# Attention and graph convolution in float32 on one core: the values' bias moved to VectorE between products, and the second half of the next x loaded into a place of the numerators

## The chip, the cores and the metric

The kernel runs on one core of one Trainium2 chip. The metric is the device time of one execution in microseconds (us), the median of the runs shown. One execution was also recorded by the hardware profiler; every instant below is in us from the start of its span. The engines are TensorE (PE; its weight loads are PEld), VectorE (DVE), ScalarE (ACT), GpSimd (POOL) and SyncE (SP), which only issues DMAs here.

## The reference

32 graphs of 512 nodes with 512 features pass through two layers, each with a residual and a layer norm:

```
q, k, v = x @ Wq + bq, x @ Wk + bk, x @ Wv + bv          # 8 heads of 64
scores  = q @ k.T / 8 + (-1e9 where adj == 0)
x = layernorm(x + softmax(scores) @ v)
norm_adj = adj * deg^-0.5[:, None] * deg^-0.5[None, :]   # deg = adj.sum(axis=1)
x = layernorm(x + norm_adj @ (x @ weight) + bias)
```

`x` is 32 x 512 x 512 in float32 and `adj` 512 x 512. Everything below is in float32 or in a high and a low part of it.

## The kernel before

`unshifted` does the work; `general` is a second version that runs only where a test at the end says that the first one's numbers left their bounds. The batch index is `b`, one graph at a time, and the two layers of different graphs are overlapped. Iteration `b` of the main loop is four stages on TensorE:

1. `stretch(b, one)`: scores of two pairs of heads, their exponentials, and the product with the values (tiles `sc`, `e`, `av`). Eight numerators `e` of 128 x 1024 lie in `NUM`; each stretch uses all eight in order, so the eighth, `NUM[:, 7]`, is written last.
2. Keys and queries of graph `b + 1` (`k0` and `k1`, 14 products taken in turn), with the layer norms of graphs `b - 1` and `b - 2` beside them.
3. `stretch(b, two)`: the other two pairs of heads.
4. `main` of 22 pieces: four of `first` (adjacency times graph `b - 1`), the values of graph `b + 1`, and `second` (times the weight of layer two).

The large products are computed with seven multiplications in place of eight (`seven` with tables such as `CHAIN`, `LEAF`, `OUTER`), from sums and differences of blocks. Those of x are made by GpSimd in `XT` by `combine` (four) and `quarters` (four more), after VectorE has transposed the two halves of x into `XT` (`turn(b, 0)` and `turn(b, 1)`). In stage 4 the values are six leaf products, a seventh, a sum on GpSimd (`spread_last`), and three outer products at positions 13, 15 and 17 of `main`; the seven products of `second` are at 10, 14, 16 and 18 to 21. The step at position n of `main` is followed by what `beside` has under n. Each of the tables' products writes a PSUM bank; the three outer ones all write the same one, region "A", and ScalarE or VectorE takes each result out (`put`, `add`) into `V[b]` or `y`. Region "A" of `second` serves its products 1, 3, 5 and 7.

Instructions keep the order in which the program names them on each engine (`keep_in_program_order`); DMAs are issued from SP in an order that the scheduler sets, and each waits at the head of the queue for what it needs. An instruction waits by semaphores for the others that write what it reads or read what it writes.

The values' bias: `bias_values(b)` adds `bv_r` to the four rows of `V[b]`, four additions of 128 x 512 on GpSimd. They stand at position 18, behind the eight combinations of x. On GpSimd the sums of numerators of the next stretch (`accumulate`, tile `acc`, six additions of 128 x 1024) follow, and behind those the roots of a layer norm (`rstd`, `add`), for which ScalarE's `store` waits (tile `y`). `store` and the evictions of keys and queries (`kq`) alternate on ScalarE.

x is loaded in two halves, four DMAs each. Both use one buffer, `x`, so the second half (`load_x(b, 1)`, called from `turn(b, 0)`) starts after the first has been transposed. Only for graph 1 does the second half lie in `NUM[:, 7]`.

Outputs of a stretch leave PSUM by a transpose on VectorE into `yb`, one buffer, and four DMAs each into `YT` (`yT<-yb`). `swap` exchanges the weights of queries and values in one tile, `wqv`.

Of the kernel before, what the change touches and what calls it, by code (L numbers as in the profile page):

```python
# [50 lines left out]
def unshifted(  # L51
# [15 lines left out]
    B, N, D = x.shape  # L67
    NT = N // P
# [5 lines left out]
    tensor, vector, scalar, gpsimd = (InOrder(tc, e) for e in (nc.tensor, nc.vector, nc.scalar, nc.gpsimd))  # L74
# [24 lines left out]
    def each(f, *args):  # L99
        return [lambda a=a: f(*a) if isinstance(a, tuple) else f(a) for a in args]  # L100

    def run(pieces):
        for f in pieces:
            f()

    def play(main, beside=None):
        for n, f in enumerate(main):
            f()
            run((beside or {}).get(n, ()))
# [11 lines left out]
        return NUM[:, next(taken) % 8]  # L121

    def load_x(b, j):
        if b == 1 and j == 1:
            X[b, j] = NUM[:, 7].rearrange("p k (n t r) -> p (k n) t r", t=DT, r=32)
        else:
            X[b, j] = acts.tile([P, 8, DT, 32], F32, name="x", bufs=1)
        for q in range(4):
            nc.sync.dma_start(
                X[b, j][32 * q : 32 * (q + 1)],  # L130
                x[b, ts(j, HALF), ts(q, P)].rearrange("(k s) (t r) -> s k t r", s=32, r=32),
            )

    def turn(b, j):
        vector.transpose(
            XT[:, 2 * j : 2 * j + 2].rearrange("p i u (k s) -> p (i u) k s", s=32),
            X.pop((b, j)).rearrange("p k t r -> p t k r"),
        )
        if j == 0 and b > 1:
            load_x(b, 1)  # L140

    turned = {}

# [75 lines left out]
    def load_row(v, name, engine):  # L219
        t = consts.tile([P, v.shape[0]], F32, name=name)  # L220
        engine.dma_start(t, bass.AP(tensor=v.tensor, offset=v.offset, ap=[[0, P], [1, v.shape[0]]]))
        return t
# [9 lines left out]
    for i in range(2):  # L232
# [3 lines left out]
        if i == 0:  # L236
            bv_r = load_row(bv, "bv_r", nc.scalar)
# [130 lines left out]
    KQ, V = {}, {}  # L368
# [50 lines left out]
        leaf = seven(LEAF, multiply_quarters, put_quarters, add_quarters, (4, P))  # L419
        return leaf + [spread_last] + seven(OUTER, multiply, put, add)  # L420

    def bias_values(b):
        for n in range(NT):
            gpsimd.tensor_add(V[b][:, n, :], V[b][:, n, :], bv_r)

    def keys_and_queries(b, r):
        def multiply(p, i, j, fresh):
            for c, w in enumerate((wk, wqv)):
                for u in range(2):
                    tensor.matmul(  # L430
                        p[:, c, :], w[:, i, u, ts(r, P)], XT[:, j, u, :],
                        start=fresh and c == 0 and u == 0, stop=u == 1, skip_group_check=True,
                    )

        def out(i, j):
            if (b, ORDER[0]) not in KQ:
                for g in ORDER:
                    KQ[b, g] = acts.tile([P, 2, N], F32, name="kq", bufs=6)
            return KQ[b, r + 2 * i][:, :, ts(j, HALF)]

        def put(q, p):
            g = r + 2 * q[0]
            for c in range(2):
                scalar.activation(out(*q)[:, c], p[:, c], AF.Identity, bias=bias[:, c, g : g + 1], scale=1.0)

        def add(q, p):
            vector.tensor_add(out(*q), out(*q), p)

        return seven(CHAIN if b else PLAIN_FIRST, multiply, put, add)
# [367 lines left out]
    v = values_of(0)  # L817
# [13 lines left out]
    weigh_quarters(gpsimd)  # L831
    nc.sync.dma_start(stored[1], NUM[:, :4].rearrange("p e k (u o) -> p (e k) u o", u=2)[:, :7])
    nc.sync.dma_start(stored[0], wqv)
    bias_values(0)
    play(keys_and_queries(0, 1), {
        1: [lambda: adjacency(0)], 3: [lambda: turn(1, 0), lambda: adjacency(1)],
    })
# [8 lines left out]
    for b in range(B):  # L846
        one, two = ORDER[:2], ORDER[2:]
        f[b], c[b] = finish(b), convolve(b)
        ahead, back = f.get(b - 1), c.get(b - 2)
        if 1 < b < LAST:  # L850
            load_residual(b - 1)
        if b + 2 < B:
            load_x(b + 2, 0)
        if b == LAST:
            load_residual(b)
        stretch(b, one, back["measure"][:3] if back else ())

        def folds(gs):
            return [[lambda g=g, b=b: fold(b, g)] for g in gs]

        def turns(b=b + 2):
            if b >= B:
                return [], [], []
            return [lambda: turn(b, 0)], [lambda: turn(b, 1)], [lambda k=k: combine(b, k) for k in range(4)] + [quarters]

        fold0, fold1 = folds(one) if b < LAST else ([], [])
        rest = back["measure"][3:] + back["root"] if back else []
        store = back["store"] if back else []
        if b < LAST:
            k0, k1 = keys_and_queries(b + 1, 0), keys_and_queries(b + 1, 1)  # L870
            main = [p for pair in zip(k0, k1) for p in pair]
            if b == 0:
                exact = each(compare, *range(NT))
                weights = each(lambda k: weigh_part(w1, gpsimd, k), *range(4))
                beside = {
                    1: fold0, 2: [degrees], 3: weights[:1], 4: fold1, 5: weights[1:2] + exact[:1], 6: exact[1:2],
                    7: weights[2:3], 8: exact[2:3], 9: weights[3:], 10: exact[3:],
                }
            else:
                measure, norm, low = ahead["measure"], ahead["norm"], ahead["low"]  # L880
                scale = ahead["inverse"] + ahead["scale"] if b == 1 else []
                beside = {
                    0: rest + scale + ahead["add"], 1: store[:1] + fold0, 2: store[1:2], 3: store[2:3] + fold1,
                    4: store[3:] + measure[:2], 5: measure[2:] + ahead["root"], 7: norm[:1] + ahead["judge"],
                    8: norm[1:2] + low[:1], 9: norm[2:3] + low[1:2], 10: norm[3:] + low[2:3],
                    11: low[3:] + ahead["lift"],
                }
            play(main, beside)
        else:
            e = f[b]  # L890
            conv = c[b - 1]
            play(conv["first"], {
                0: rest + store[:1] + conv["parts"][:0], 1: store[1:2] + ahead["judge"] + conv["parts"][:1],
                2: store[2:] + e["sums0"],
                3: conv["parts"][1:] + e["inverse0"] + ahead["grow"],
            })

        if b < LAST:
            swap(1)
        stretch(b, two, f[b]["pairs"][0] + f[b]["pairs"][1] if b == LAST else ())  # L900

        fold0, fold1 = folds(two) if b < LAST else ([], [])
        turn0, turn1, combined = turns()
        if b < LAST:
            end = f[b]
            v, bias_v = values_of(b + 1), [lambda b=b + 1: bias_values(b)]
            back_to_queries = [lambda: swap(0)] if b < LAST - 1 else []
            if b == 0:
                play(v, {
                    1: fold0, 4: fold1, 8: turn0, 9: turn1, 10: combined + back_to_queries + bias_v,  # L910
                })
            else:
                conv = c[b - 1]
                second = conv["second"]
                k = 6 if b < LAST - 1 else 8
                main = conv["first"] + v[:k] + second[:1] + v[k:9] + second[1:2] + v[9:10] + second[2:3] + v[10:] + second[3:]
                grow, parts, scale = ahead["grow"], conv["parts"], end["scale"]
                if b < LAST - 1:
                    beside = {
                        1: parts[:1] + fold0, 3: parts[1:], 5: fold1, 6: grow[:1], 8: grow[1:2], 9: grow[2:3] + end["inverse"],  # L920
                        10: grow[3:] + scale[:1], 11: scale[1:2], 13: turn0 + scale[2:3], 14: scale[3:],
                        16: turn1, 17: combined[:2], 18: combined[2:] + back_to_queries + bias_v,
                    }
                else:
                    measure, norm, low = end["measure"], end["norm"], end["low"]
                    beside = {
                        0: [lambda: load_residual(LAST - 1)], 1: parts[:1] + fold0, 3: parts[1:], 5: fold1,
                        6: grow[:1], 8: grow[1:2], 9: end["inverse"], 10: grow[2:3] + scale[:2], 11: grow[3:] + scale[2:] + end["add"],
                        14: measure[:1], 15: measure[1:2], 16: measure[2:3],
                        17: measure[3:] + end["root"], 18: norm[:1] + bias_v, 19: norm[1:2] + low[:1], 20: norm[2:3] + low[1:2],  # L930
                        21: norm[3:] + low[2:] + end["lift"],
                    }
                play(main, beside)
# [312 lines left out]
```

## Time and profile before

| | |
|---|---|
| median of 3 runs | 2786.29 us (2782.73 to 2787.06) |
| the profiled execution | 2788.38 us, its span 2786.6 us |
| granted TensorE clock | 0.995 |
| one iteration in the middle, from one restart of TensorE in stage 2 (1015.90) to the next (1100.97) | 85.07 us |
| TensorE's products of stage 4 in that iteration | 1040.55 to 1071.84 |
| scores and av after it | 1071.84 to 1085.93 |
| keys and queries | 1085.93 to about 1111.5 |
| the additions `v<-v,bv_r` on GpSimd | 128, 1300 ns each in the mean, 161.8 us |
| GpSimd's additions of 128 x 1024, `acc<-acc,e` | 248, 2373 ns each |
| VectorE's turn of half an x, `xT<-x` | 61, 1242 ns each |

A profile line gives the start, the time, the engine, the operation and what it writes and reads, its shape and count; in square brackets is how long the engine sat idle before it and what ended that. In the list of waits the numbers are us in total, how often, and the longest. In the chain of waits each step is what released the next. Ends of TensorE's products are modelled: a group of four is shown longer than the distance to the next one.

### The profile page before, as it was taken

Reading aid. Unit: us, or ns where it says so; the run is one execution under the profiler, and the core shown is the slowest. Engines: PE = TensorE matmul, PEld = TensorE weight load, DVE = VectorE, ACT = ScalarE, POOL = GpSimd, SP = SyncE. Lnnn points to the kernel's source line nnn. Section 1 sums busy time; section 2 is a strip of 40 time slices with the busy share of each in tenths; the row PEclk is TensorE's granted clock in tenths of the full one; section 3 lists DMA queues with packets and bytes.
Section 4 is the critical chain, followed back from the end, with each engine's and each line's share of the span. In section 5 each row is a group of like instructions: output and inputs, shape, how many; then the busy total and the mean of one; then the engine's idle time right before and its main releaser. Section 6 shows DMA issues by size and latency. Waiting matters only on the chain.

```text
span 2786.6 us, 36220 instructions
## 1 busy us (share of the span) xinstructions
PE 2717.3 (98%) x13284; PEld 1907.6 (68%) x13284; DVE 1972.3 (71%) x2809; ACT 1257.0 (45%) x1807; POOL 1999.4 (72%) x1335
## 2 busy tenths in 40 slices
PE   9899999999999999999999999999999999999997
PEld 6566766766767667667667676676676676766765
DVE  4767767677676777776676767777777767677777
ACT  3344434454344544344543445443545434454444
POOL 5667676687776776766877767767668777677674
PEclk9999999999999999999999999999999999999999
DMA  5213333233333233332333332333323333323321
GB/s 178 80 45 109 99 86 101 77 94 106 88 98 103 61 111 90 95 102 74 97 106 88 96 99 68 110 88 94 106 68 103 106 87 95 96 71 110 93 59 47
DMA packets 388187, 256.76 MB, mean 92 GB/s; under 512 B 278816, under 2 KB 346400, under 8 KB 379936
## 3 DMA queue, kind: packets, MB, share of 16 engines
q1 hardware_dynamic: 386848, 252.78, 30.5%
q8 instruction: 107, 1.75, 0.3%
q10 hardware_dynamic: 1152, 1.57, 0.2%
q14 instruction: 80, 0.66, 0.1%
HBM read 183.77 MB, written 37.22 MB: 79 GB/s over the span
## 4 chain that ended last, share of the span: by engine, by line
PE 76%; DVE 8%; POOL 5%; ACT 4%; DMA 3%; SPq 2%; issue 1%; ACTq 0%; DVEq 0%; POOLq 0%
PE mm L45 48%; PE sc L45 15%; PE av L45 13%; POOL acc L45 2%; ACT kq L45 2%; DMA yT<-yb 2%; SPq L512 2%; ACT y L45 1%; DVE yb L45 1%; DVE folded L45 1%; DVE acc L45 1%; DVE ve L45 1%; POOL rstd L45 1%; POOL xT L45 1%; DVE st L45 1%
## 5 line engine op out<-in xcount | busy, mean ns | idle before, releaser
L45 ACT ACTIVATE e<-e 128x1024 f32<-128x1024 f32 x512 | 541.3, 1057 | 599.6 <-DVE e L45 566.7
L45 DVE SCALAR_TENSOR_TENSOR e<-sc,maskT 128x1024 f32<-128x1024 f32 x512 | 584.9, 1214 | 64.6 <-PE sc L45 64.6
L45 POOL TENSOR_TENSOR acc<-acc,e 128x1024 f32<-128x1024 f32 x248 | 588.5, 2373 | 19.4
L45 PE MATMUL mm<-xT,wk 128*128 128x256 f32 x1792 | 466.5, 383 | 32.5 <-ACT kq L45 32.5
L45 POOL TENSOR_TENSOR xT<-xT 128x512 f32<-128x512 f32 x250 | 314.2, 1273 | 243.2 <-DVE xT L45 233.4
L45 PE MATMUL sc<-kq 64*128 64x512 f32 x2048 | 459.8, 597 | 2.8 <-DVE e L45 1.4
L45 PE MATMUL av<-e,v 128*64 128x512 f32 x2048 | 456.9, 598 | 5.2 <-POOL v L45 4.9
L45 PE MATMUL mm<-xT,wqv 128*128 128x256 f32 x1792 | 459.9, 379 | 0.0
L45 PEld LDWEIGHTS mm<-xT,wk 128*128 128x128 f32 x1792 | 334.9, 190 | 113.4 <-ACT kq L45 44.1
L45 PEld LDWEIGHTS mm<-xT,wqv 128*128 128x128 f32 x1792 | 340.5, 190 | 46.3
L45 PEld LDWEIGHTS av<-e,v 128*64 128x64 f32 x2048 | 145.3, 137 | 309.4 <-issue 232.4
L45 PEld LDWEIGHTS sc<-kq 64*128 64x128 f32 x2048 | 191.8, 186 | 238.9 <-issue 182.0
L45 ACT ACTIVATE kq<-mm,bias 128x256 f32<-128x256 f32 x512 | 213.9, 472 | 234.7 <-PE mm L45 232.1
L45 PE MATMUL mm<-wqv,xT 128*128 128x128 f32 x1736 | 304.8, 322 | 5.8 <-DVE v L45 5.8
L45 POOL TENSOR_TENSOR acc<-e 128x1024 f32<-128x1024 f32 x126 | 298.1, 2366 | 17.4 <-ACT e L45 17.4
L45 POOL TENSOR_TENSOR yT<-yT,b_r 128x512 f32<-128x512 f32 x126 | 157.2, 1281 | 212.4 <-DVE lo L45 212.4
L45 PEld LDWEIGHTS mm<-wqv,xT 128*128 128x128 f32 x1736 | 263.4, 192 | 30.0 <-issue 4.6
L45 DVE STREAM_TRANSPOSE yb<-av 128x512 f32<-128x512 f32 x127 | 91.1, 717 | 259.4 <-DMA yT<-yb 191.9
L45 DVE TENSOR_TENSOR v<-v,mm 128x512 f32<-128x512 f32 x221 | 147.5, 679 | 151.0 <-PE mm L45 146.3
L45 PE MATMUL mm<-w,zT 128*128 128x256 f32 x992 | 229.5, 379 | 0.0
L45 DVE STREAM_TRANSPOSE acc<-acc 128x1024 f32<-128x1024 f32 x124 | 152.6, 1231 | 77.1 <-POOL acc L45 76.8
L45 PEld LDWEIGHTS mm<-w,zT 128*128 128x128 f32 x992 | 186.1, 190 | 24.8 <-issue 0.8
(133 smaller groups left out, 3446.6 us busy)
## 6 DMA issues: line engine op xcount, KB each, us to landing
wqv<-wv_parts SPq DMA_DIRECT2D x31, 1792.0 KB, 7.5
wqv<-wq_parts SPq DMA_DIRECT2D x30, 1792.0 KB, 7.5
yT<-yb SPq DMA_DIRECT2D x508, 64.0 KB, 2.3
x<-in_x_dram SPq DMA_DIRECT2D x244, 128.0 KB, 3.2
out_dram<-y SPq DMA_DIRECT2D x120, 256.0 KB, 2.0
xr<-in_x_dram SPq DMA_DIRECT2D x118, 256.0 KB, 3.6
wk<-in_x_dram SPq DMA_DIRECT2D x8, 256.0 KB, 2.8
wv_parts<-e SPq DMA_DIRECT2D x1, 1792.0 KB, 7.6
```

The source lines that it names most:

```text
L45: return self.tc.keep_in_program_order(op(*args, **kwargs))
L512: nc.sync.dma_start(YT[b][:, :, (4 * g + q) * 32 : (4 * g + q + 1) * 32], yb[32 * q : 32 * (q + 1)],)
```

## The change

Three things change in iterations of the main loop.

- `turn` no longer loads the second half. `load_x(b + 2, 1)` is called once in iteration `b`, after `stretch(b, two)`, and puts the second half into `NUM[:, 7]`, for every graph.
- `bias_values` adds one row and takes an engine. For the values of graphs 2 to 30, iterations 1 to 29, VectorE adds the four rows, after positions 17, 18, 19 and 20 of `main`, each in front of an addition of `second`. In iterations 0 and 30 and for graph 0 GpSimd still does it.
- In iterations 1 to 29 the second turn moves from position 16 to 14, ahead of the last scaling and of the addition of the second outer product. GpSimd's combinations follow it after 14, 15 and 17; `swap(0)` goes from 18 to 17.

```diff
@@ load_x @@
-        if b == 1 and j == 1:
+        if j == 1:
             X[b, j] = NUM[:, 7].rearrange("p k (n t r) -> p (k n) t r", t=DT, r=32)
@@ turn @@
             X.pop((b, j)).rearrange("p k t r -> p t k r"),
         )
-        if j == 0 and b > 1:
-            load_x(b, 1)
@@ bias_values @@
-    def bias_values(b):
-        for n in range(NT):
-            gpsimd.tensor_add(V[b][:, n, :], V[b][:, n, :], bv_r)
+    def bias_values(b, n, engine=gpsimd):
+        engine.tensor_add(V[b][:, n, :], V[b][:, n, :], bv_r)
...
-    bias_values(0)
+    run(each(bias_values, *((0, n) for n in range(NT))))
...
         turn0, turn1, combined = turns()
+        if b + 2 < B:
+            load_x(b + 2, 1)
         if b < LAST:
             end = f[b]
-            v, bias_v = values_of(b + 1), [lambda b=b + 1: bias_values(b)]
+            v, bias_v = values_of(b + 1), each(bias_values, *((b + 1, n) for n in range(NT)))
...
                 if b < LAST - 1:
+                    bias_v = each(bias_values, *((b + 1, n, vector) for n in range(NT)))
                     beside = {
                         1: parts[:1] + fold0, 3: parts[1:], 5: fold1, 6: grow[:1], 8: grow[1:2], 9: grow[2:3] + end["inverse"],
-                        10: grow[3:] + scale[:1], 11: scale[1:2], 13: turn0 + scale[2:3], 14: scale[3:],
-                        16: turn1, 17: combined[:2], 18: combined[2:] + back_to_queries + bias_v,
+                        10: grow[3:] + scale[:1], 11: scale[1:2], 13: turn0 + scale[2:3], 14: turn1 + scale[3:] + combined[:1],
+                        15: combined[1:2], 17: combined[2:] + bias_v[:1] + back_to_queries, 18: bias_v[1:2],
+                        19: bias_v[2:3], 20: bias_v[3:],
                     }
```

## The prediction

> **What bounds the kernel now.** I read the page first, then the waits, the chain of waits over one middle batch, and each engine's timeline over that batch (iteration 11's values, then iteration 12's keys and queries). Busy time of the engines, from the page:
>
> ```profile
> PE 2717.3 (98%) x13284; PEld 1907.6 (68%) x13284; DVE 1972.3 (71%) x2809; ACT 1257.0 (45%) x1807; POOL 1999.4 (72%) x1335
> ```
>
> TensorE is the bound: only 69 us of the span are left to win unless products change, and none do. What TensorE waits for (sum, times, longest):
>
> ```profile
> PE mm L45 <- ACT kq L45: 32.5, 29, 1.6
> PE mm L45 <- DVE v L45: 5.8, 4, 3.6
> PE av L45 <- POOL v L45: 4.9, 1, 4.9
> ```
>
> One wait in each of 29 batches holds half of it. The chain of waits shows where it comes from (start, length):
>
> ```profile
> 1092.89 2.35 POOL acc L45
> 1095.23 0.98 POOL rstd L45
> ...
> 1098.06 0.70 ACT y L45
> 1098.76 0.73 ACT kq L45 x2
> 1099.49 0.70 ACT y L45
> 1100.19 0.74 ACT kq L45 x2
> 1100.93 0.04 issue
> 1100.97 10.63 PE mm L45 x48
> ```
>
> GpSimd's sums of the numerators (acc) end late, the root (rstd) queues behind them, ScalarE's first output row (y) waits for the root, and the keys' evictions (kq) queue behind y. The ninth product of the stage wants the bank that the fifth one's eviction empties. GpSimd's timeline says why acc is late:
>
> ```profile
> 1065.56 10.36 POOL L45 TENSOR_TENSOR xT<-xT 128x512 f32<-128x512 f32 x8 [6.96 <-DVE xT L45]
> 1075.88 4.98 POOL L45 TENSOR_TENSOR v<-v,bv_r 128x512 f32<-128x512 f32 x4
> 1080.83 2.37 POOL L45 TENSOR_TENSOR acc<-e 128x1024 f32<-128x1024 f32 x1
> ```
>
> The numerators were there from about 1076.5 (ScalarE's exponentials begin at 1074.28, 1.12 apart, two are needed). Acc begins at 1080.83 because of x's late second half and the bias.
>
> **What the Trainium skill says.** "SBUF — State Buffer", section "Who interferes with whom": a VectorE instruction with two SBUF inputs and a GpSimd instruction that reads SBUF exclude each other, and the later one waits for the whole of the other. The bias on VectorE is such an instruction. The trace agrees; the timeline of the first batch has the same shape, 128x512 from two SBUF inputs, beside four GpSimd additions:
>
> ```profile
> 79.57 5.86 POOL L45 TENSOR_TENSOR w<-w 128x512 f32<-128x512 f32 x4
> 80.25 1.15 DVE L45 TENSOR_TENSOR plainT<-plainT,adjT 128x512 f32<-128x512 f32 x1
> 82.62 1.67 DVE L45 TENSOR_TENSOR plainT<-plainT,adjT 128x512 f32<-128x512 f32 x1
> 86.12 0.69 DVE L45 TENSOR_TENSOR plainT<-plainT,adjT 128x512 f32<-128x512 f32 x1
> ```
>
> Alone it takes 0.69. Beside GpSimd it ends some 0.56 after GpSimd's addition: the first of the four ends at 79.57+1.27=80.84, VectorE at 80.25+1.15=81.40. The second, held back by about 0.46, ends near 82.57, and VectorE, which comes at 82.62, just misses that gap and waits for the third: 1.67. GpSimd's next one, held back, takes about 1.72 (the first v,bv_r additions, from 28.59, last 3.39 for two beside VectorE's) instead of 1.27.
>
> **The change, part by part.** VectorE's order around the outer products decides (v are the values' additions from PSUM, y the second factor's):
>
> ```profile
> 1058.20 0.69 DVE L45 TENSOR_TENSOR v<-v,mm 128x512 f32<-128x512 f32 x1 [0.73 <-PE mm L45]
> 1058.81 1.24 DVE L45 STREAM_TRANSPOSE xT<-x 128x1024 f32<-128x1024 f32 x1
> 1059.97 0.65 DVE L45 TENSOR_TENSOR yT<-yT,inv 128x512 f32<-128x512 f32 x1
> 1060.54 0.68 DVE L45 TENSOR_TENSOR y<-yT,mm 128x512 f32<-128x512 f32 x1
> 1061.14 0.68 DVE L45 TENSOR_TENSOR yT<-yT,inv 128x512 f32<-128x512 f32 x1
> 1061.74 0.68 DVE L45 TENSOR_TENSOR v<-v,mm 128x512 f32<-128x512 f32 x1
> 1063.31 0.69 DVE L45 TENSOR_TENSOR y<-yT,mm 128x512 f32<-128x512 f32 x1 [0.90 <-PE mm L45]
> 1064.17 1.25 DVE L45 STREAM_TRANSPOSE xT<-x 128x1024 f32<-128x1024 f32 x1 [0.17 <-DMA x<-in_x_dram]
> ```
>
> *The load.* Four DMAs of 128 KB into the eighth numerator. They wait for GpSimd's last sum of that place, which ends at 1045.7 (six sums from 1031.16), not for the first turn, and land near 1053 (3.2 from issue to landing). In the built order of the SP queue two of them stand ahead of the second four yT<-yb transfers, which before went out at 1043.2. These now leave after 1046.6 and land before 1052; they are wanted by the first scaling at 1056.2. That cover of 4 us makes it cost nothing. Were acc to end 5 us later, it would show. swap(0) and the residual wait for TensorE (1065.0, 1072.1) as before.
>
> *The second turn earlier.* It goes from 1064.17 to 1061.17, straight behind y, then the last scaling, then the addition of the second outer product at 1061.17+1.16+0.60=1062.93 instead of 1061.74. That addition has a customer: all three outer products use one bank, and the third product waits for it (the same wait, 0.85, stands twice in the first batch, at 119.82 and 122.67, each 0.75 after its addition began). The third product begun at 1063.11; it will begin at 1062.93+0.75=1063.68. **Loss 0.57 per batch**, 29 x 0.57 = 16.5 us. Nothing hides it: TensorE has no other work in its order.
>
> *GpSimd.* The eight xT combinations start near 1062.9; the third waits for the third outer product (about 1065.7). With the bias interleaved they end near 1075, and 4.98 us of bias are gone. Acc can begin when the exponentials permit, 4.3 us earlier than at 1080.83 on the same scale. The root then starts near 1091.3 instead of 1095.2; ve, which needs GpSimd to be between two sums, is ready at 1089.4 and ends by 1091.2. First y at 1092.7, then kq, y in turn (0.72 each): the fifth kq ends near 1097. TensorE needs it at 1099.8. **The wait goes whole**, with 2.8 us to spare. Its worth: idle 32.5/29=1.12, and 0.16 that the modelled ends hide (groups of four matmuls start 0.865 apart: 1098.98+0.865=1099.84, next start 1100.97, so 1.13 lost where 0.97 is shown): 29 x 1.28 = 37.2 us. Next on that path would be the product itself.
>
> *The bias on VectorE.* 29 x 4 additions of 0.69. Between the y additions, one per TensorE product of 1.73, 1.04 are free. Against GpSimd's additions each pair runs as a cycle: GpSimd held back 1.72, VectorE's bias ending 0.56 after the boundary, y in between. 1.72 fits 1.73. So what counts is whether the first bias catches the boundary between the third and fourth combination. Counted from the third outer product's end E: VectorE starts the third product's two v additions at E+0.20 (its y starts 0.20 after each product, 1068.49 for 1068.29), they last 1.25, and bias needs their result (0.04 more, as between a turn of acc and its sum), so it is ready at E+1.49. GpSimd's third combination starts between E+0.22 and E+0.31 (parts started 0.31 after the last product that reads its place) and ends at E+1.49 to E+1.58. Caught, on the scale of this batch with the 0.57 of delay in it: the four biases end at 1067.55, 1069.30, 1071.03 and 1072.77, the last y at 1073.37, and the scores permit e at 1073.59 (1073.02+0.57): cost 0. Missed: each of them is some 1.2 later, the y of the fifth product of the second factor ends at 1071.1, and the seventh, which adds to the same bank and would start at 1070.6, starts 0.55 late: 29 x 0.55 = 16 us. Both ends kept; I take caught, since a GpSimd start of 0.31 is what the trace has.
>
> *First batch.* GpSimd keeps its bias there, but the second turn waited 2.41 for x. It comes 2.5 earlier, and so do the bias and the av products that waited 4.9 for it: gain 2.5 us (the wait of sc is upstream of it and not added).
>
> Sum on the profiled execution (2788.4 us, span 2786.6): 2788.4 - 37.2 + 16.5 - 2.5 = 2765.2. The median of the runs is 2.1 below that execution: **2763 us**.
>
> **Rivals.**
> - *The boundary is missed.* 16 us more: 2779. For it: a tie within 0.1 us. Against: the 0.31 above.
> - *The outer product does not wait*, because VectorE gets there sooner than my addition of rows: 2763 - 16.5 = 2747. Against: the rows are 0.6 pitched throughout.
> - *A convoy at the shared port: slower.* If held-back GpSimd additions take 1.9 instead of 1.72, a bias-y cycle exceeds the 1.73 of a product and lateness adds up, 0.2 a turn; with a missed boundary the last y and e come some 0.9 late. The scores have little slack: e pitch 1.14 against 0.88 for a pair of products, four pairs of banks to run ahead in. Price 0.57+0.55+0.9=2.0 a batch, 58 us, against gains of 39.7: 2786.3+18=2804. It decides from 1.37 us a batch. For it: nearly touching schedules; against: 1.71 to 1.74 where the two engines alternated.
> - *No change*: the missed boundary with a larger outer wait (1.3 a batch), about 2785.
>
> **How the numbers follow.** Caught boundary 0.48, missed 0.24, no outer wait 0.08, no change 0.08, convoy 0.12. 0.2% (5.6 us, about what a measurement of this kernel can tell) puts the missed case mostly, not wholly, among the faster ones. Faster 0.76, same 0.12, slower 0.12. Range 2746 to 2783.
>
> **What will show it.** PE mm <- ACT kq gone from the waits; a PE mm <- DVE v of about 0.4 to 0.6, 29 times; v<-v,bv_r on DVE with a mean near 1.15 (0.56 after the boundary), 1.2 to 1.7 for the first one if missed; xT on POOL with a mean near 1.5; acc starting 4.7 after the first scores. I am wrong if kq's wait stays, if sc waits for DVE e, or if yT<-yb's new place on SP shows up before a scaling.

## The result and the profile after

The changed kernel takes 2761.62 us (median of 6 runs, 2760.66 to 2762.93), the kernel before beside it 2785.93 (6 runs). The ratio is 0.9915, with a 95% interval from 0.9902 to 0.9928: 0.85% faster. The profiled execution took 2760.92 us, its span is 2759.1.

The busy line of the page of the changed kernel, then two lines from its list of what TensorE waited for (total, times, longest):

```profile
PE 2715.4 (98%) x13284; PEld 1907.3 (69%) x13284; DVE 2075.0 (75%) x2925; ACT 1259.6 (46%) x1807; POOL 1910.7 (69%) x1219
```

```profile
PE mm L45 <- DVE v L45: 15.2, 33, 3.6
...
PE av L45 <- POOL v L45: 4.0, 2, 3.8
```

TensorE's own work is the same. The line for ScalarE's kq, 32.5 us in 29 batches before, is gone from the list. In its place the wait for VectorE's v has risen from 4 occurrences to 33: a new one in each of the same 29 batches, 0.32 us shown each time. VectorE's busy time rises by 103 us and GpSimd's falls by 89, and neither is the bound.

GpSimd's timeline of the changed kernel in the same iteration 11 (start, time, operation; in brackets the idle time before it):

```profile
1051.10 2.90 POOL L45 TENSOR_TENSOR xT<-xT 128x512 f32<-128x512 f32 x2 [3.92 <-DVE xT L45]
...
1054.26 9.36 POOL L45 TENSOR_TENSOR xT<-xT 128x512 f32<-128x512 f32 x6 [0.25 <-PE mm L45]
...
1065.71 2.37 POOL L45 TENSOR_TENSOR acc<-e 128x1024 f32<-128x1024 f32 x1 [2.10 <-ACT e L45]
```

The sums of numerators now wait for ScalarE's exponentials for 2.10 us, where before they came late. They begin 4.70 us after the first scores (1061.01); before it was 8.99 (1080.83 against 1071.84). So ScalarE's alternation of y and kq starts early too. Two lines from its timeline in the changed kernel:

```profile
1081.57 0.82 ACT L45 ACTIVATE y<-y,add,rstd 128x512 f32<-128x512 f32 x1 [1.87 <-POOL add L45]
...
1085.12 0.84 ACT L45 ACTIVATE kq<-mm,bias 128x256 f32<-128x256 f32 x2
```

The second of them is the fifth eviction of keys and queries. It ends at 1085.96; the ninth product of the stage, which needs its bank, starts at 1089.02. There are 3 us to spare where there was a wait.

The chain of waits shows what has become late instead (start, length of each step):

```profile
1046.79 0.69 DVE v L45
1047.47 1.00 DVE xT L45
...
1048.58 0.62 DVE yT L45
1049.20 0.60 DVE y L45
1049.80 0.40 DVE xT L45
...
1050.88 0.65 DVE yT L45
1051.53 0.61 DVE v L45
...
1052.18 8.90 PE mm L45 x40
```

Reading from the bottom: TensorE's third outer product starts at 1052.18, released by VectorE's addition of the second one, which stood behind a scaling, the second turn, y, another scaling and the first turn, without a gap. TensorE's own timeline in the same stretch:

```profile
1049.97 1.89 PE L45 MATMUL mm<-w,parts 128*128 128x256 f32 x8
1052.18 1.99 PE L45 MATMUL mm<-wqv,xT 128*128 128x256 f32 x8 [0.32 <-DVE v L45]
1054.01 1.89 PE L45 MATMUL mm<-w,zT 128*128 128x256 f32 x8
```

Without the wait the outer product would have started one pitch, 1.73 us, after the one before it: 1049.97 + 1.73 = 1051.70. So it is 0.48 late, of which the list shows 0.32, because the modelled end of the product before it hides the rest.

Last, VectorE's and GpSimd's meeting at the bias (VectorE's timeline):

```profile
1054.21 1.28 DVE L45 TENSOR_TENSOR v<-v,mm 128x512 f32<-128x512 f32 x2 [1.49 <-PE mm L45]
...
1055.53 0.69 DVE L45 TENSOR_TENSOR v<-v,bv_r 128x512 f32<-128x512 f32 x1
...
1056.14 0.68 DVE L45 TENSOR_TENSOR y<-y,mm 128x512 f32<-128x512 f32 x1
1056.74 1.16 DVE L45 TENSOR_TENSOR v<-v,bv_r 128x512 f32<-128x512 f32 x1
...
1061.18 0.67 DVE L45 TENSOR_TENSOR y<-yT,mm 128x512 f32<-128x512 f32 x1
...
1062.19 4.62 DVE L45 SCALAR_TENSOR_TENSOR e<-sc,maskT 128x1024 f32<-128x1024 f32 x4 [0.34 <-PE sc L45]
```

GpSimd's third combination begins at 1054.26 and, at its 1.27, ends at 1055.53. This end is the boundary of which the prediction speaks. The first bias begins at that very instant and takes 0.69, as if alone; GpSimd's fourth combination begins 0.08 later, at 1055.61. So it is in all 29 batches. The next three biases take about 1.16, each waiting for the end of one combination. The last y ends at 1061.85, 0.34 before e can begin: the scores are not delayed.

### The profile page after: what moved, and what is told of

It is laid out like the page before. It is cut to its first block, busy times and chain, and to the rows that moved or that the text cites. A ratio compares the mean times of both kernels' runs of the same rounds, so it can differ in the third digit from the quotient of the medians.

```text
span 2759.1 us, 36196 instructions
## 1 busy us (share of the span) xinstructions
PE 2715.4 (98%) x13284; PEld 1907.3 (69%) x13284; DVE 2075.0 (75%) x2925; ACT 1259.6 (46%) x1807; POOL 1910.7 (69%) x1219
## 3 DMA queue, kind: packets, MB, share of 16 engines
q8 instruction: 107, 1.75, 0.3%
## 4 chain that ended last, share of the span: by engine, by line
PE 90%; DVE 7%; issue 1%; POOL 1%; ACT 0%; DMA 0%; SPq 0%; DVEq 0%; POOLq 0%; ACTq 0%
PE mm L45 58%; PE av L45 16%; PE sc L45 16%; DVE xT L45 2%; DVE yT L45 2%; DVE v L45 2%; DVE y L45 1%; POOL xT L45 0%; DVE st L45 0%; DVE lo L45 0%; ACT yT L45 0%; ACT hi L45 0%; DVE e L45 0%; POOL y L45 0%; DMA xr<-in_x_dram 0%
## 5 line engine op out<-in xcount | busy, mean ns | idle before, releaser
L45 POOL TENSOR_TENSOR xT<-xT 128x512 f32<-128x512 f32 x250 | 369.0, 1486 | 156.9 <-DVE xT L45 139.8
L45 PE MATMUL mm<-wqv,xT 128*128 128x128 f32 x1736 | 306.5, 322 | 15.2 <-DVE v L45 15.2
L45 PE MATMUL mm<-adjT,hi 128*128 128x512 f32 x512 | 201.6, 397 | 0.8 <-ACT e L45 0.8
```

The source lines that it names most:

```text
L45: return self.tc.keep_in_program_order(op(*args, **kwargs))
```

## The experiments

Seven kernels were run, each beside the kernel before (2786.05 and 2786.32 in the two groups). The edits are shown against the changed kernel, that of e2 against the kernel before; `...` stands for code that is left out. The table has the time, what TensorE waited for in the profile (shown us, times), and how long after the first scores of one middle batch acc began.

| kernel | us (runs) | <- ACT kq | <- DVE v | <- DVE y | acc after scores |
|---|---|---|---|---|---|
| before | 2785.93 (6) | 32.5, 29 | 5.8, 4 | none | 8.99 |
| the change | 2761.62 (6) | none | 15.2, 33 | none | 4.70 |
| e1 bias back on GpSimd | 2760.00 (4) | none | 15.1, 33 | none | 5.91 |
| e2 bias alone | 2750.48 (4) | none | 6.0, 4 | 1.2, 4 | 5.46 |
| e3 turn one place later | 2762.46 (4) | none | 5.9, 4 | 9.8, 28 | 4.75 |
| e4 short sum ahead of the bias | 2762.00 (4) | none | 15.2, 33 | none | 4.70 |
| e5 bias and load, turn where it was | 2743.48 (4) | none | 6.0, 4 | none | 5.23 |
| e6 load alone | 2771.46 (4) | 20.9, 29 | 5.9, 4 | none | 8.71 |
| e7 longer sum ahead of the bias | 2784.60 (12) | none | 15.2, 33 | 14.4, 29 | 4.75 |

**e1: is it the bias leaving GpSimd that pays?**

```diff
-                    bias_v = each(bias_values, *((b + 1, n, vector) for n in range(NT)))
-                        15: combined[1:2], 17: combined[2:] + bias_v[:1] + back_to_queries, 18: bias_v[1:2],
-                        19: bias_v[2:3], 20: bias_v[3:],
+                        15: combined[1:2], 17: combined[2:] + back_to_queries, 18: bias_v,
```

> The change with the four additions of the bias put back on GpSimd behind the combinations of x; the early load and the early second turn stay. My theory: what matters is only that the sums of numerators start at least 1.3 us sooner than before. GpSimd's combinations now end about 7.8 us after the third of them starts, the bias about 5 us later, so acc starts some 6.1 us after the first scores, where it was 9.0 before and is 4.7 in the change. That is enough: PE mm <- ACT kq stays at zero, PE mm <- DVE v stays near 0.3 shown (0.5 in truth) in 29 batches, time 2762 (2759 to 2766), the same as the change. Rival, that the bias leaving GpSimd is what pays: kq's wait comes back in part or whole, 2775 to 2799.

It took 2760.00, ratio to before 0.9904 (0.9888 to 0.9921), against 0.9915 (0.9902 to 0.9928) for the change: the intervals of the ratios overlap, so no difference is claimed. GpSimd's timeline of this run:

```profile
1054.17 7.78 POOL L45 TENSOR_TENSOR xT<-xT 128x512 f32<-128x512 f32 x6 [0.24 <-PE mm L45]
1061.90 4.97 POOL L45 TENSOR_TENSOR v<-v,bv_r 128x512 f32<-128x512 f32 x4
1066.83 2.37 POOL L45 TENSOR_TENSOR acc<-e 128x1024 f32<-128x1024 f32 x1
```

Six combinations that nobody holds back take 7.78, not 9.36, and the bias 4.97 more; acc begins only 1.2 later, relative to the scores, than in the change. That is still early enough, and the wait for kq stays away. With x turned early, the bias need not leave GpSimd at all. The rival falls.

**e2: the bias alone.** x is loaded and turned as in the kernel before, and the four rows of the bias go to VectorE as in the change (`bias_values` and its other calls are those of the change too).

```diff
+                    bias_v = each(bias_values, *((b + 1, n, vector) for n in range(NT)))
...
-                        16: turn1, 17: combined[:2], 18: combined[2:] + back_to_queries + bias_v,
+                        16: turn1, 17: combined + bias_v[:1] + back_to_queries, 18: bias_v[1:2],
+                        19: bias_v[2:3], 20: bias_v[3:],
```

> The kernel before with the bias alone moved to VectorE between the second factor's products; x is loaded and turned as before. My theory: acc starts about 3 us sooner than before (GpSimd's eight combinations, four of them held back by 0.46, end near 12.1 us after their start, and no bias follows), so PE mm <- ACT kq is gone; and the second outer product's addition is not delayed, so PE mm <- DVE v is back at 4 occurrences. Gain 37 of before: 2749 (2746 to 2753), faster than the change by 12. Rival, that the additions on VectorE cost what they delay (PSUM banks freed late, e late): 2760 or more, with PE sc <- DVE or PE mm <- DVE y waits in every batch.

It took 2750.48 (2748.10 to 2752.27), ratio 0.9871 (0.9855 to 0.9888): inside what was expected, and faster than the change. Each of the two moves, the early turn in e1 and the bias here, removes the wait for kq by itself; the one of the bias does so without the new wait for v.

**e3: the second turn one place later**, behind the second outer product's addition.

```diff
-                        ... 14: turn1 + scale[3:] + combined[:1],
-                        15: combined[1:2], 17: combined[2:] + bias_v[:1] + back_to_queries, 18: bias_v[1:2],
+                        ... 14: scale[3:],
+                        15: turn1 + combined[:2], 17: combined[2:] + bias_v[:1] + back_to_queries, 18: bias_v[1:2],
```

> The change with the second turn moved one place later, from behind position 14 to behind 15, so that the second outer product's addition comes before it. My theory: the third outer product no longer waits for it, 29 x 0.5 = 14 us back: 2748, with PE mm <- DVE v at 4 occurrences. But the first bias now comes within 0.1 us of GpSimd's boundary behind its second combination; if it misses, the seventh product of the second factor starts some 0.5 late and the time is 2762 again, with PE mm <- DVE y 29 times. Rival, that the wait for DVE v hides something else that ends just as late: about 2760 with another wait in its place.

It took 2762.46, the time of the change, but not by the same wait: the one for v is back at 4, and one for y stands in 28 batches. Its timeline, both engines and TensorE:

```profile
1053.31 11.80 POOL L45 TENSOR_TENSOR xT<-xT 128x512 f32<-128x512 f32 x8 [5.11 <-DVE xT L45]
...
1055.95 1.75 DVE L45 TENSOR_TENSOR v<-v,bv_r 128x512 f32<-128x512 f32 x1
...
1060.13 1.97 PE L45 MATMUL mm<-w,zT 128*128 128x256 f32 x8 [0.35 <-DVE y L45]
```

GpSimd starts its combinations at a moment that is bad for the bias: its third one begins at 1055.89, 0.06 before the bias, which then waits for all of it and takes 1.75. The y behind it come later, and the seventh product of `second` waits for the fifth one's addition to their common bank. This was the second outcome named in the expectation.

One of the 29 batches of this run went the other way, and it is the test of the boundary within one kernel:

```profile
295.92 0.83 DVE L45 TENSOR_TENSOR v<-v,bv_r 128x512 f32<-128x512 f32 x1
```

There the combination on GpSimd had still 0.28 us to run when the bias asked. The bias took 0.83 instead of 1.74 to 1.76, TensorE did not wait for y, and from the scores behind the batch before it to those behind it 83.92 us went by, against 84.48 to 84.57 for the 27 batches that follow. GpSimd starts some 0.3 later in the same batch of e2 and e5 too; why was not found out.

**e4 and e7: does the boundary decide?** A sum that nothing uses is put on VectorE ahead of the first bias, in e4 over 128 x 4, in e7 over 128 x 384 (`bv_r[:, :384]` in the place of `minus_half`).

```diff
+    def nudge():
+        t = small.tile([P, 1], F32, name="nudge")
+        vector.tensor_reduce(t, minus_half, AX.X, ALU.add)
...
-                        15: combined[1:2], 17: combined[2:] + bias_v[:1] + back_to_queries, 18: bias_v[1:2],
+                        15: combined[1:2], 17: combined[2:] + [nudge] + bias_v[:1] + back_to_queries, 18: bias_v[1:2],
```

> The change with one small sum of 128 x 4 on VectorE, about 0.19 us, ahead of the first bias in each of the 29 batches; it computes nothing that is used. My theory: the first bias then comes just after GpSimd's fourth combination began, waits for it, lasts about 1.6 instead of 0.69, all later ones move with it by 1.0 to 1.2, and the seventh product of the second factor waits about 0.5 for VectorE's fifth addition to its bank: 2762 + 12 to 16 = 2774 to 2778. Rival, that VectorE has room there and the order of the two engines doesn't matter: 2762 to 2763.

e4 took 2762.00: my expectation missed by 12 to 16 us. VectorE's timeline says why:

```profile
1054.07 1.28 DVE L45 TENSOR_TENSOR v<-v,mm 128x512 f32<-128x512 f32 x2 [1.49 <-PE mm L45]
...
1055.27 0.15 DVE L45 TENSOR_REDUCE nudge<-minus_half 128x1 f32<-128x4 f32 x1
1055.39 0.69 DVE L45 TENSOR_TENSOR v<-v,bv_r 128x512 f32<-128x512 f32 x1
```

The bias reads what the two v additions write, and begins 0.04 after their end at 1055.35, as in the change (1055.53 after 1055.49). The sum doesn't read it: it began 0.08 before their end and was over, at 1055.42, just behind the bias's start. Nothing was moved, so nothing was tested; e7 has a sum that is longer than the gap.

> The change with a longer sum on VectorE (128 x 384, about 0.5 us) ahead of the first bias; the shorter one ran in the 0.12 us in which the bias waits for VectorE's own result and moved nothing. My theory: the bias is then ready some 0.45 after GpSimd's boundary, waits for the fourth combination, lasts about 1.4, the later ones move by about 1.2, and TensorE waits for DVE y some 0.35 to 0.4 shown (0.5 in truth) in 29 batches, as in the kernel with the turn one place later: 2762 + 14 = 2774 to 2778. Rival, that the boundary doesn't matter for the change: 2762, or less than 5 us more.

e7 took 2784.60 (12 runs, 2782.26 to 2786.24), ratio to before 0.9994 (0.9985 to 1.0003): the whole gain of the change is gone. Its timeline:

```profile
1060.44 9.33 POOL L45 TENSOR_TENSOR xT<-xT 128x512 f32<-128x512 f32 x6 [0.25 <-PE mm L45]
1061.60 0.55 DVE L45 TENSOR_REDUCE nudge<-bv_r 128x1 f32<-128x384 f32 x1
...
1062.06 1.55 DVE L45 TENSOR_TENSOR v<-v,bv_r 128x512 f32<-128x512 f32 x1
...
1066.03 1.97 PE L45 MATMUL mm<-w,zT 128*128 128x256 f32 x8 [0.49 <-DVE y L45]
```

The boundary was at 1060.44 + 1.27 = 1061.71; the bias came at 1062.06, 0.35 late, and had to wait for the fourth combination. The 0.55 us of VectorE's own work is not the cost as such. The bias ends at 1063.61, 0.55 after the fourth combination (1063.06), just as in e3, which adds no work and where the bias ended 0.55 after the combination that it waited for; and TensorE waits for y in 29 batches, as it does in 28 of e3. The mechanism is the expected one and the price, put at 2774 to 2778, is larger: the product starts at 1066.03 instead of 1063.65 + 1.73 = 1065.38, so 0.65 a batch, and 0.1 for the restart of TensorE (see the next part). 29 x 0.75 = 22, which is what the two profiled executions differ by (2782.97 less 2760.92).

**e5: the two parts without the early turn.**

```diff
-                        ... 14: turn1 + scale[3:] + combined[:1],
-                        15: combined[1:2], 17: combined[2:] + bias_v[:1] + back_to_queries, 18: bias_v[1:2],
+                        ... 14: scale[3:],
+                        16: turn1, 17: combined + bias_v[:1] + back_to_queries, 18: bias_v[1:2],
```

> The change with the second turn at position 16, as in the kernel before; the early load and the bias on VectorE stay. My theory: the wait of the third outer product goes (29 x 0.48 = 14 us against the change), GpSimd's sums still start early enough, the second turn never waits for x, so the first bias always catches its boundary with 0.2 us to spare, and the first batch keeps its 2.5 us: 2745 to 2748, 2 to 5 faster than the bias alone (2750). Rival, that the early load brings nothing beyond the early turn: 2750, with the bias alone.

It took 2743.48 (2742.72 to 2745.91), ratio to before 0.9850 (0.9834 to 0.9867): the fastest of all, somewhat better than expected, 18 us below the change and 7 below the bias alone; the rival falls. Its timeline:

```profile
1046.45 11.81 POOL L45 TENSOR_TENSOR xT<-xT 128x512 f32<-128x512 f32 x8 [6.70 <-DVE xT L45]
1047.51 0.76 DVE L45 TENSOR_TENSOR v<-v,bv_r 128x512 f32<-128x512 f32 x1
...
1053.24 0.67 DVE L45 TENSOR_TENSOR y<-yT,mm 128x512 f32<-128x512 f32 x1
...
1054.16 9.14 DVE L45 SCALAR_TENSOR_TENSOR e<-sc,maskT 128x1024 f32<-128x1024 f32 x8 [0.26 <-PE sc L45]
```

The first combination ends at 1046.45 + 1.27 = 1047.72 and the bias asks at 1047.51: it catches the boundary with 0.21 to spare, and the last y ends at 1053.91, before e begins. In e2, where the turn waits for its x, TensorE waited for y in four batches (0.19 to 0.42 us each, the 1.2 us of the table), though no bias there took longer than 1.16, so no boundary was missed. The trace of e2 shows what it was:

```profile
1472.09 1.25 DVE L45 STREAM_TRANSPOSE xT<-x 128x1024 f32<-128x1024 f32 x1 [0.97 <-DMA x<-in_x_dram]
...
1477.72 1.97 PE L45 MATMUL mm<-w,zT 128*128 128x256 f32 x8 [0.42 <-DVE y L45]
```

The second turn waited for x 0.74, 0.80, 0.83 and 0.97 us in these four batches, and TensorE then for y 0.19, 0.26, 0.29 and 0.42: always 0.54 to 0.55 less. In the other batches whose bias VectorE adds the turn waited 0.68 or less, and no wait for y is listed. (At 0.68 there is a small one that the list leaves out: the last two products of `second` take 4.00 together, and 3.62 in a batch where the turn waited 0.18.) So a late x pushed the turn, and all of VectorE's work behind it, back; the early load takes that away.

**e6: the load alone.**

```diff
-                    bias_v = each(bias_values, *((b + 1, n, vector) for n in range(NT)))
-                        ... 14: turn1 + scale[3:] + combined[:1],
-                        15: combined[1:2], 17: combined[2:] + bias_v[:1] + back_to_queries, 18: bias_v[1:2],
-                        19: bias_v[2:3], 20: bias_v[3:],
+                        ... 14: scale[3:],
+                        16: turn1, 17: combined[:2], 18: combined[2:] + back_to_queries + bias_v,
```

> The early load alone: second turn at position 16 and the bias on GpSimd, as in the kernel before. My theory: GpSimd's chain comes sooner only by the turn's wait for x (0.17 in most batches, 2.4 in the first), and each 0.1 of it takes 0.1 off the wait for kq: 29 x 0.2 to 0.35 = 6 to 10 us, and 2.5 in the first batch: 2773 to 2778. kq's wait stays, about 0.8 to 1.0 shown, 29 times. Rival, that the load by itself is worth nothing (hidden): 2783 to 2787; rival, that the load is what pays: 2765 or less.

It took 2771.46, ratio 0.9948 (0.9931 to 0.9965), a little better than expected. One line of its waits:

```profile
PE mm L45 <- ACT kq L45: 20.9, 29, 0.7
```

The wait is shorter by 11.6 us in total (0.40 a batch), and acc comes 0.43 earlier after the scores in the mean of the 29 batches (8.71 against 9.14); of this 0.32 is the mean time that the turn had waited for its DMA, and the rest stays open. With the first batch's 2.5 the sum is 14.1 of the 14.9 measured. The batches of the kernel before show the same among themselves: acc 8.99 after the scores goes with a wait of 0.97, acc 9.46 with 1.47; only above that does the wait grow no further (acc 9.83, wait 1.54). So from 8.7 to 9.5 the wait for kq follows GpSimd's start nearly one for one.

## Why the prediction was right

The forecast was 2763 and the measurement is 2761.6. The mechanism was the forecast one, a wait removed and a smaller one made; in one step the forecast had luck. By its steps:

- *The wait for kq goes whole, with 2.8 us to spare.* It went, with 3.0 to spare. e1 and e2 show that the lateness of GpSimd was its cause: two different ways to make it earlier each remove it, and e6, which makes it earlier by too little, shortens it.
- *The third outer product waits 0.57.* It starts 0.48 late and pays 0.1 more to restart, 0.58 in all. The profile shows 0.32 of it, less than the 0.4 to 0.6 that the prediction wanted to see. e2 and e5, which leave the turn where it was, are back at 4 occurrences; e5 less the change is 18.1 us, and 29 x 0.58 = 16.8 of it.
- *The restart* was in neither term of the sum: a group of products after a wait takes 0.97 to the next group and not 0.865. The wait for kq was worth 1.28 + 0.1, the new one 0.48 + 0.1. In the difference it cancels: 0.80 a batch, and one iteration is shorter by 0.78 (85.25 to 84.47 in the mean of 28).
- *The first bias catches the boundary.* It did, by nothing, and that was luck: it begins at the instant at which the combination ends, 0.08 before GpSimd takes its next one. The forecast rested on GpSimd starting 0.31 after its product; it was 0.25. As the first bias did not have to wait at all, the mean of the four is 1.04 and not near 1.15.
- *The missed boundary costs 16 us.* It wasn't met, but e7 shows 22: 2784.6, where the prediction had 2779. This term was too small, by the restart and by 0.1 of the wait. Had GpSimd started a tenth of a microsecond sooner, the change might have measured as no change. That so small a shift is enough is shown by e3, where the bias misses by 0.06; that it would cost the change the whole 22 us is argued from e7, not shown.
- *The load's place on the SP queue costs nothing.* The second four `yT<-yb` went out from 1035.21 to 1037.86, after two of the x; the scaling at 1044.77 did not wait. No run took this place away.
- *The first batch gains 2.5.* Its av began at 134.95 instead of 138.07, of which 0.61 was there before stage 4's second outer product (119.21 against 119.82): 2.5.
- *A convoy at the port.* It did not form: the pairs of bias and y recur every 1.68, inside the 1.73 of a product.

## What to carry to other kernels

A gain on the engine that was late is worth only what its last customer still waits for: here some 1.3 us of earlier sums in the mean batch, the size of the wait, would have been enough; this is an estimate from the one-for-one of e6. 4.3 were won, the surplus bought nothing (e1 won 3.1 and took the same time), and the addition that was pushed back for it cost 0.58 of the 1.38 us that each batch had gained. When work is moved on an in-order engine, look at each instruction that is pushed back and at who waits for it; moving the second turn from 16 to 14 cost 18 us against e5, which is the same kernel without it. Where two engines exclude each other, compare the instants at which they ask: 0.08 us on the good side in the change and 0.06 on the bad side in e3 decided whether TensorE waited in nearly every batch.

## What was not expected of the hardware

- TensorE paid about 0.1 us beyond the wait itself when it restarted: the first product of eight after a wait for v is shown with 1.99 instead of 1.89, and the next starts 1.83 and not 1.73 later. It isn't the products' wait alone. The same 0.97 in place of 0.865 stands at the start of the keys and queries (1075.10 to 1076.07 in the change), where no idle time of the products is shown, but the load of the first weights had waited. In both places the first product begins together with the load of its weights; in the running stream the load begins some 0.21 ahead (1098.77 for the product of 1098.98 in the kernel before). That this late load is the price is likely, not shown.
- A VectorE instruction that read nothing pending began 0.08 before the shown end of the one before it, while one that read its result began 0.04 after that end (e4). So 0.15 us of added work moved nothing in 29 batches.
- The Trainium skill, "SBUF — State Buffer", section "Who interferes with whom", has a VectorE instruction with two SBUF inputs and a GpSimd instruction that reads SBUF exclude each other. The traces agree, with sizes that repeat closely: an addition of 128 x 512 on VectorE took 0.69 on a free port, 1.16 in each of the three later biases, 1.55 to 1.75 when it had missed a boundary, and ended 0.55 after the combination that it waited for. GpSimd's combinations lost less than VectorE's 0.69: six of them took 9.36 beside three waiting biases and one free, 7.78 beside none, so 0.40 for each of the four.
- At the boundary the engine that came first got the port, even when it came by less than 0.1 us: the bias won in the 29 batches of the change, 0.08 before GpSimd's next combination began, and lost in 28 batches of e3, 0.06 to 0.07 after it had begun.
